# Layer 0 of a four-layer network: the output projection of a chunk and the power of its norm, issued half a turn sooner

## The chip, the cores and the metric

The kernel runs on one core of a Trainium2 chip. A core has five engines that run side by side, each with its own queue: PE (TensorE, matrix products; its weight loads are listed apart as PEld), DVE (VectorE), ACT (ScalarE), POOL (GpSimd) and SP (SyncE, which here only issues DMAs). Engines wait for one another through semaphores. The metric is the device time of one execution in microseconds (us).

## The reference, cut to what matters

The network takes x of shape 16 x 64 x 64 x 256 (16 images of 4096 pixels with 256 channels) and adds four layers to it, one after the other, each as `x = x + layer(group_norm(x))`. The change lies in layer 0, which is a linear attention:

```python
qkv = jnp.einsum('bhwc,cf->bhwf', x, Wqkv)            # x is the group-normed input
q = jax.nn.softmax(q, axis=-3); k = jax.nn.softmax(k, axis=-2)
context = jnp.einsum('bdnh,benh->bdeh', k, v)         # per head
out = jnp.einsum('bdeh,bdnh->benh', context, q)
out = jnp.einsum('bhwc,cf->bhwf', out, Wout) + bout   # the output projection
out = (out - mean(out)) * rsqrt(var(out) + 1e-6) * ln_scale + ln_bias
```

The mean over the 256 output channels is taken out of `Wout` and `bout` beforehand, so the norm of the projection needs only the mean of the squares, a power of -1/2, and a scaling. Layers 1 to 3 are not touched.

## The kernel before, in words

**Tiles and turns.** An image is cut into 8 chunks of 512 pixels (`NCH`, `CT`), and the 256 attention channels into two halves `hf`. Layer 0 is one loop of turns (line 565): turn n treats image i, half hf and chunk t, with n = 16 i + 8 hf + t, and after the last of these 256 turns there are 16 more that finish the last image. A turn computes q, k and v of its chunk and half (`attended`). The images are overlapped: while (i, hf) is in `attended`, the softmax and the context of the half before it are worked off by generators in the list `chains` (`context`, `weighted`, `gate1`, `norm0`), which `step()` advances five times a turn. `output` multiplies the context into the weighted q in parts that are due in turns t = 3 to 7.

**The projection.** The turns with hf = 1 also project one chunk of the image before (`projected0`, job "x1"). So 8 turns of 16 carry a projection, 128 in the layer; the last image's chunks are projected two to a turn after the last q turn. One projection is:

- 8 products of `o` with `wo` into the PSUM tile `py` (line 424; each is two PE instructions, 16 in all);
- DVE adds `bout`, which gives `y` (line 429);
- ACT squares `y` in four quarters, with a sum of each (line 433);
- DVE scales the four sums and adds epsilon, `ss` (line 434); POOL raises it to -1/2, `rsy` (line 436);
- ACT scales `y` by `rsy`, four instructions (line 439);
- PE transposes `y` into two tiles `pt` (line 444; 16 instructions); ACT applies scale and bias, `yT` (line 448); DVE adds the input and takes maximum and statistics (lines 451 and 455). A store of the result is queued for the next turn.

`projected0` is a generator with a `yield` between these pieces. The loop advances it at fixed points. Call the turn in which a chunk's projection begins k. At the start of turn k the generator is made and run to its first `yield` (lines 588 to 591). In `between(0)` of turn k, which `attended` calls after the q product and the first half of the k and v products, the loop runs it on (lines 603 and 604). At the start of turn k+1 it is run on once more (lines 583 and 584), and in `between(0)` of turn k+1 for the last time (lines 601 and 602).

**PSUM.** Tag `mm` has two buffers of two banks: `pkv` (k and v), `py`, and `px` (line 502, the transposes of `mapped`, in some turns only) take them in turn. Tag `tr` has three one-bank buffers, for `pq`, `po` and `pt`. Tag `sm` has one, for the small products of the chains. In SBUF, `y` has three buffers, which it shares with the tile `mx` of the maximum tree in `context`.

**Order.** There is no hand-written instruction order. The framework lays out each engine's instructions at build time: the order of the text is the priority, and an instruction whose inputs its cost model holds for late lets a later one pass. On the chip each engine keeps the order laid out. The trace shows both: six of the sixteen instructions of `py` sometimes run ahead of the transposes `pt` of the chunk before, which the text has first.

Of the kernel before, what the change touches and what calls it, by code (L numbers as in the profile page):

```python
# [36 lines left out]
def network(ctx: ExitStack, tc: tile.TileContext, a: dict, out: bass.AP):  # L37
# [142 lines left out]
    with ExitStack() as st:  # L180
# [232 lines left out]
        def projected0(i, ch):  # L413


            if ch == 0:
                st1[i] = wk.tile([P, 2, NCH, 6], F32, tag="st1", name="st1")
                mxs[i] = wk.tile([P, 2, NCH], F32, tag="mxs", name="mxs")
            x1 = loaded.pop(("x1", i, ch))
            yield  # L420
            py = mm.tile([P, 4, C], F32, tag="mm", name="py")
            for q in range(4):
                for hf in range(2):
                    nc.tensor.matmul(  # L424
                        py[:, q, :], lhsT=om[i, hf][:, :, ch * 4 + q], rhs=wo[:, hf, :],
                        start=(hf == 0), stop=(hf == 1),
                    )
            y = wk.tile([P, 4, C], F32, tag="y", name="y", bufs=3)
            nc.vector.tensor_tensor(y, py, bout.unsqueeze(1).broadcast_to([P, 4, C]), ALU.add)
            ss = small.tile([P, 4], F32, tag="ss", name="ss")  # L430
            sq = wk.tile([P, C], F32, tag="sq", name="sq", bufs=1)
            for q in range(4):
                nc.scalar.activation(sq, y[:, q, :], AF.Square, accum_out=ss[:, q : q + 1])
            nc.vector.tensor_scalar(ss, ss, 1.0 / C, LN_EPS, ALU.mult, ALU.add)
            rsy = small.tile([P, 4], F32, tag="rsy", name="rsy")
            nc.gpsimd.tensor_tensor(rsy, ss, mhalf, ALU.pow)
            yield
            for q in range(4):
                nc.scalar.activation(y[:, q, :], y[:, q, :], AF.Copy, scale=rsy[:, q : q + 1])
            yield  # L440
            for h in range(2):
                pt = tr.tile([P, CT], F32, tag="tr", name="pt")
                for q in range(4):
                    nc.tensor.transpose(
                        pt[:, q * P : (q + 1) * P], y[:, q, h * P : (h + 1) * P], ident
                    )
                t = wk.tile([P, CT], F32, tag="t", name="yT", bufs=4)
                nc.scalar.activation(
                    t, pt, AF.Identity, bias=lnb[:, h : h + 1], scale=lns[:, h : h + 1]
                )  # L450
                nc.vector.tensor_tensor_reduce(
                    x1[:, h], t, x1[:, h], 1.0, -3.0e38, ALU.add, ALU.max,
                    accum_out=mxs[i][:, h, ch : ch + 1],
                )
                nc.vector.bn_stats(st1[i][:, h, ch, :], x1[:, h])
            stores.append(
                (x1_d[i, :, :, ch * CT : (ch + 1) * CT].rearrange("h p t -> p h t"), x1)
            )
            if ch == NCH - 1:
                chains.append(gate1(i))  # L460
# [104 lines left out]
        for n in range(LAST + 16):  # L565
# [22 lines left out]
            for job in work:  # L588
                if job[0] == "x1":
                    projecting.append(projected0(*job[1:]))  # L590
                    next(projecting[-1])
# [1058 lines left out]
```

## Time and profile before

| | us |
|---|---|
| median of three runs (8559.8 to 8580.07) | 8560.48 |
| the profiled execution, its own time | 8603.53 |
| its span, first to last instruction | 8601.7 |
| layer 0 in it (the last transposes of the last image's chunks are still running at 3096) | about 3110 |

| Engine | busy us in the span | share |
|---|---|---|
| PE | 6924.3 | 80% |
| PEld | 5146.2 | 60% |
| DVE | 6022.7 | 70% |
| ACT | 4835.8 | 56% |
| POOL | 3054.3 | 36% |

The median and the profiled execution differ by 43 us (0.5%). A profile page gives busy time per engine; what stands behind a waiting engine is read from the list of waits, in which a line says who waited for whom, for how many us in total, how often, and how long at most. A line of the timeline gives start, duration, engine, line, operation, the tiles written and read, the number of merged instructions, and in brackets the engine's idle time before it with what ended it. In the rows by stretches, each engine has its busy time in the stretch and the number of its instructions; then come the granted TensorE clock as a share of full speed, the share of DMA engines in use and the GB/s moved.

### The profile page before, as it was taken

Reading aid. Unit: us, or ns where it says so; the run is one execution under the profiler, and the core shown is the slowest. Engines: PE = TensorE matmul, PEld = TensorE weight load, DVE = VectorE, ACT = ScalarE, POOL = GpSimd, SP = SyncE. Lnnn points to the kernel's source line nnn. Section 1 sums busy time; section 2 is a strip of 40 time slices with the busy share of each in tenths; the row PEclk is TensorE's granted clock in tenths of the full one; section 3 lists DMA queues with packets and bytes.
Section 4 is the critical chain, followed back from the end, with each engine's and each line's share of the span. In section 5 each row is a group of like instructions: output and inputs, shape, how many; then the busy total and the mean of one; then the engine's idle time right before and its main releaser. Section 6 shows DMA issues by size and latency. Waiting matters only on the chain. (4 is left out here: it accounts for less than half of the span.)

```text
span 8601.7 us, 215728 instructions
## 1 busy us (share of the span) xinstructions
PE 6924.3 (80%) x88348; PEld 5146.2 (60%) x88348; DVE 6022.7 (70%) x7839; ACT 4835.8 (56%) x11136; POOL 3054.3 (36%) x2154
## 2 busy tenths in 40 slices
PE   7888888888888776477777777778588888888888
PEld 5666666666666542254555555555376767777776
DVE  6777777777766757499999999999744444444444
ACT  3555555555555536666666656665355555555554
POOL 1222222222222200367777777777611112111112
PEclk9999999999999868799888888889799999999999
DMA  6543333443333327756767677676578878888887
GB/s 221 180 141 133 133 128 133 142 137 130 130 113 108 101 80 244 234 188 230 241 230 239 229 232 236 228 240 195 173 222 257 248 243 255 252 258 252 252 256 241
DMA packets 1081775, 1695.70 MB, mean 197 GB/s; under 512 B 138834, under 2 KB 684963, under 8 KB 1079635
## 3 DMA queue, kind: packets, MB, share of 16 engines
q1 hardware_dynamic: 1080786, 1681.90, 60.7%
q8 instruction: 696, 11.40, 0.6%
q14 instruction: 293, 2.39, 0.1%
HBM read 1234.54 MB, written 469.76 MB: 198 GB/s over the span
## 5 line engine op out<-in xcount | busy, mean ns | idle before, releaser
L1107 DVE TENSOR_TENSOR pd<-xs,pw 128x1152 f32<-128x1152 f32 x1024 | 1305.3, 1346 | 5.3 <-ACT xs L1088 5.3
L1367 PE MATMUL pk<-rt,span 64*128 64x176 f32 x12288 | 1179.9, 328 | 51.3 <-issue 44.9
L1122 POOL TENSOR_TENSOR pd<-pd 128x2048 f32<-128x2048 f32 (+2 forms) x384 | 1066.8, 2778 | 314.6 <-DVE pd L1107 294.5
L1377 ACT ACTIVATE wm<-pk,spanb 128x176 f32<-128x176 f32 x2560 | 847.0, 425 | 554.8 <-PE pk L1367 551.5
L1453 POOL TENSOR_TENSOR ex<-ex,rx 128x192 f32<-128x192 f32 (+2 forms) x768 | 436.3, 571 | 1855.3 <-DVE ex L1446 1152.3
L1367 PEld LDWEIGHTS pk<-rt,span 64*128 64x128 f32 x12288 | 969.4, 191 | 128.2 <-issue 69.8
L292 PE MATMUL pkv<-wq,xn 128*128 128x256 f32 x4096 | 1000.8, 390 | 49.4 <-DVE isq L93 27.6
L1446 DVE SCALAR_TENSOR_TENSOR ex<-pa,msk,ex 128x192 f32<-128x192 f32 x704 | 294.0, 418 | 1056.9 <-ACT ex L1445 984.2
L292 PEld LDWEIGHTS pkv<-wq,xn 128*128 128x128 f32 x4096 | 792.2, 196 | 280.5 <-issue 154.0
L375 POOL TENSOR_TENSOR qa<-qa,mq 128x1024 f32<-128x1024 f32 x256 | 493.7, 1950 | 1295.0 <-DVE mq L387 633.8
L1433 PE MATMUL pa<-wm,xw 126*32 126x48 f32 x45056 | 762.9, 214 | 221.7 <-issue 179.8
L1382 DVE TENSOR_TENSOR wm<-pk,spanb 128x704 f32<-128x704 f32 x896 | 793.8, 888 | 187.6 <-PE pk L1367 185.7
L1433 PEld LDWEIGHTS pa<-wm,xw 126*32 126x32 f32 x45056 | 626.7, 111 | 411.5 <-issue 332.8
L1038 PE MATMUL px<-x2p,wis 128*128 128x512 f32 x1024 | 581.7, 717 | 196.1 <-ACT c L1136 130.2
L1084 PE MATMUL pt<-ident,pad 128*128 128x128 f32 x4608 | 613.6, 287 | 129.0 <-ACT rt L1062 76.4
L1084 PEld LDWEIGHTS pt<-ident,pad 128*128 128x128 f32 x4608 | 522.8, 147 | 287.9 <-ACT rt L1062 97.2
L1088 ACT COPY xs<-pt 128x512 f32<-128x512 f32 x1152 | 591.4, 601 | 138.5 <-PE pt L1084 129.8
L1258 DVE TENSOR_REDUCE x<-pd 128x512 f32<-128x4608 f32 x128 | 633.4, 4948 | 1.9
L280 PE MATMUL pq<-xn,wq 128*128 128x512 f32 x1024 | 525.3, 629 | 29.0 <-ACT xn L165 22.6
L424 PE MATMUL py<-wo,o 128*128 128x256 f32 x2048 | 533.0, 409 | 4.2 <-DVE maps L510 1.9
L1445 ACT ACTIVATE ex<-pa,msk 128x192 f32<-128x192 f32 x704 | 299.8, 426 | 413.0 <-PE pa L1433 219.4
L424 PEld LDWEIGHTS py<-wo,o 128*128 128x128 f32 x2048 | 488.2, 309 | 30.3 <-issue 5.6
(233 smaller groups left out, 11870.8 us busy)
## 6 DMA issues: line engine op xcount, KB each, us to landing
xw<-strips SPq DMA_DIRECT2D x1408, 256.0 KB
xn<-in_x SPq DMA_DIRECT2D x256, 512.0 KB
x_d<-x SPq DMA_DIRECT2D x256, 512.0 KB
xin<-in_x SPq DMA_DIRECT2D x128, 512.0 KB
x<-in_x SPq DMA_DIRECT2D x128, 512.0 KB
xm<-x_d SPq DMA_DIRECT2D x128, 512.0 KB
x<-x_d SPq DMA_DIRECT2D x128, 512.0 KB
x<-x_d SPq DMA_DIRECT2D x256, 256.0 KB
```

Of the source, the lines that this page charges most:

```text
L292: nc.tensor.matmul(pkv[:, q], lhsT=xn[:, h, q * P : (q + 1) * P], rhs=wq[:, h, f0 + P : f0 + 384], start=(h == 0), stop=(h == 1),)
L424: nc.tensor.matmul(py[:, q, :], lhsT=om[i, hf][:, :, ch * 4 + q], rhs=wo[:, hf, :], start=(hf == 0), stop=(hf == 1),)
L1038: nc.tensor.matmul(px, lhsT=w[:, h, fh * P : (fh + 1) * P], rhs=x2[:, h], start=(h == 0), stop=(h == 1),)
L1084: nc.tensor.transpose(pt[:, k, h * P : (h + 1) * P], lines[:, h, rc * 4 + e + k, 2 * j : 2 * j + P], ident,)
L1088: nc.scalar.copy(xs[:, e : e + 2, j, :], pt)
L1107: nc.vector.tensor_tensor(pd[:, r].rearrange("p (g f) k -> p g f k", f=16), run[:, oh * 9 * P : (oh + 1) * 9 * P].rearrange("p (g f k) -> ...
L1122: nc.gpsimd.tensor_tensor(pd[..., 0:n], pd[..., 0:n], pd[..., n : 2 * n], ALU.add)
L1258: nc.vector.tensor_reduce(x3[:, :, P:C], pd1, AX.X, ALU.add)
L1367: nc.tensor.matmul(pkv[:, b, m], lhsT=span[half, first + gg, s0 : s0 + P], rhs=rto[half, o // 4 * 2 + m, :], start=True, stop=True,)
L1377: nc.scalar.activation(dst[:, m // 2, m % 2], pkv[:, m // 2, m % 2], AF.Identity, bias=spanb[:, g0 + m : g0 + m + 1],)
L1382: nc.vector.tensor_tensor(dst, pkv, spanb[:, g0 : g0 + 4].rearrange("p (b m) -> p b m", b=2).unsqueeze(3).broadcast_to([P, 2, 2, NTL]), AL ...
L1433: nc.tensor.matmul(pav[p0 : p0 + 32, :, tj * TC : (tj + 1) * TC].rearrange("c g (w v) -> c g w v", v=2), lhsT=xw[0:TILE_IN, k, tj, 32 * q ...
```

## The change

In `projected0` the first `yield`, between taking the loaded input and the products into `py`, is removed, and a second `yield` is put behind the power. So the products, the addition of `bout`, the squares, `ss` and `rsy` are issued at the start of turn k, after the chains' first step, after the scaling of the chunk before and after the first transposition `qT` of the turn, but before the q, k and v products of the turn. The advance in `between(0)` of turn k then does nothing. Scaling (start of turn k+1) and transposes (`between(0)` of turn k+1) stay where they were. No instruction is added, removed or resized.

```diff
@@ -417,7 +417,6 @@
                 st1[i] = wk.tile([P, 2, NCH, 6], F32, tag="st1", name="st1")
                 mxs[i] = wk.tile([P, 2, NCH], F32, tag="mxs", name="mxs")
             x1 = loaded.pop(("x1", i, ch))
-            yield
             py = mm.tile([P, 4, C], F32, tag="mm", name="py")
             for q in range(4):
                 for hf in range(2):
@@ -434,6 +433,7 @@
             nc.vector.tensor_scalar(ss, ss, 1.0 / C, LN_EPS, ALU.mult, ALU.add)
             rsy = small.tile([P, 4], F32, tag="rsy", name="rsy")
             nc.gpsimd.tensor_tensor(rsy, ss, mhalf, ALU.pow)
+            yield
             yield
             for q in range(4):
                 nc.scalar.activation(y[:, q, :], y[:, q, :], AF.Copy, scale=rsy[:, q : q + 1])
```

## The prediction, made before the result was known

> **What bounds the kernel now.** I read the busy times by stretches first, because the page's shares are means over four layers and the change touches only the first.
>
> ```profile
> 320.00:800.00 480.00, 409.58 (x2849) 303.12 (x2847) 363.04 (x559) 267.03 (x470) 111.43 (x71) 0.95 0.46 152
> 800.00:2800.00 2000.00, 1747.03 (x12045) 1313.88 (x12046) 1448.38 (x2220) 1131.26 (x2086) 450.71 (x298) 0.95 0.38 128
> 2962.00:3125.00 163.00, 101.01 (x648) 78.50 (x647) 119.87 (x204) 72.64 (x167) 29.16 (x20) 0.74 0.37 122
> 3125.00:8601.00 5476.00, 4271.03 (x70106) 3159.99 (x70104) 3774.76 (x4383) 3129.49 (x8019) 2369.06 (x1702) 0.90 0.72 231
> ```
>
> After the start, layer 0 is PE's: in 2000 us of its middle PE is busy 1747 us (87%), DVE 72%, ACT 57%, POOL 23%, and DMA engines are 38% in use. What can be gained is PE's idle 253 us there. The last row, 5476 us of layers 1 to 3, is out of reach of the change. The list of PE's waits in the same 2000 us says what the idle time is:
>
> ```profile
> PE pt L444 <- ACT y L439: 96.5, 71, 2.7
> PE pk L331 <- DVE mx L315: 36.5, 11, 3.4
> PE pctx L350 <- issue: 25.8, 21, 2.6
> PE pkv L292 <- DVE isq L93: 21.8, 8, 3.2
> ```
>
> The largest wait, 38% of the idle time, is that of the transposes of the projection for the scaled y. The view of tile y gives it for the whole layer: 148.0 us in 106 waits, of which 30.0 lie before 800 us and 19.6 after 2962. For its cause I read the timeline of one ordinary turn with a projection (idle time in brackets).
>
> ```profile
> 1221.92 1.21 DVE L429 TENSOR_TENSOR y<-py,bout 128x1024 f32<-128x1024 f32 x1
> ...
> 1223.83 0.42 ACT L433 ACTIVATE sq<-y 128x256 f32<-128x256 f32 x1
> ...
> 1226.80 0.19 ACT L433 ACTIVATION_READ_ACCUMULATOR sq<-y 128x1 f32 x1
> ...
> 1227.10 0.17 DVE L434 TENSOR_SCALAR ss<-ss 128x4 f32<-128x4 f32 x1 [3.97 <-ACT sq L433]
> ...
> 1227.34 1.27 POOL L436 TENSOR_TENSOR rsy<-ss,mhalf 128x4 f32<-128x4 f32 x1 [10.96 <-DVE ss L434]
> 1227.44 0.60 PE L424 MATMUL py<-wo,o 128*128 128x256 f32 x2
> ...
> 1228.65 1.71 ACT L439 ACTIVATE y<-y,rsy 128x256 f32<-128x256 f32 x4 [0.82 <-POOL rsy L436]
> ...
> 1229.21 0.84 PE L444 MATMUL pt<-ident,y 128*128 128x128 f32 x4 [1.17 <-ACT y L439]
> ```
>
> It is one chain over four engines: py ends on PE at 1221.6, then addition, squares, sums, power, first scaling, and the first transpose starts at 1229.2, 7.6 us later. PE has only 6.4 us of other work to put in between (1221.6 to 1228.04), so it stands still for 1.17 us. At the change of image the chain is longer:
>
> ```profile
> 1264.49 2.29 DVE L387 TENSOR_REDUCE mq<-qa 128x64 f32<-128x2048 f32 x1 [3.34 <-ACT qa L284]
> ...
> 1266.69 0.16 DVE L434 TENSOR_SCALAR ss<-ss 128x4 f32<-128x4 f32 x1
> ...
> 1266.86 1.91 POOL L375 TENSOR_TENSOR qa<-qa,mq 128x1024 f32<-128x1024 f32 x1 [12.98 <-DVE ss L434]
> ...
> 1268.73 1.19 POOL L436 TENSOR_TENSOR rsy<-ss,mhalf 128x4 f32<-128x4 f32 x1
> ...
> 1270.51 1.44 PE L444 MATMUL pt<-ident,y 128*128 128x128 f32 x6 [2.40 <-ACT y L439]
> ```
>
> Here the sums lie behind a maximum of `weighted`, which itself waited for the q copy, and the power behind a subtraction of `weighted` on POOL. PE waits 2.4 us, and 2.7 us again for the next chunk. PE's waits for the scaled y in one image are 0.9 us (from 1178 to 1206), 3.7 (1206 to 1256) and 5.1 (1256 to 1291): 9.7 us.
>
> **What the Trainium skill says.** "Perfetto Trace Analysis", section Optimization Strategy: find the gaps on the engine that limits, see which semaphore ends them, and make that dependency start sooner. That is what the change does to the largest gap above. "TensorE: Matmul & The Clock Gate", section Architectural detail: ACT and DVE are strict first-in first-out, and PE can pull only weight loads ahead. The trace agrees: the sums at 1266.69 did not pass the maximum ahead of them, and PE stood still at 1229.21 with products of py queued behind the transposes. Same page, section What's actually happening: the array's clock is throttled by default and activity releases the throttle. The trace shows 1.00 granted from 1206 to 1256, where waits are near 1 us, and 0.92 from 1256 to 1277. So I expect no loss of clock from shorter gaps, and count no gain. "SBUF — State Buffer", section on its two separate sides: DVE and GpSimd share a port pair, held for whole instructions. The sums took 1.09 us at 1285.69, beside a subtraction on POOL, against a median of 0.169.
>
> **The change part by part.** Nothing is added or removed. Moved, 128 times: 16 py instructions (3.84 us of PE in a row), the addition (1.21), four squares with their reads (4 x (0.42 + 0.19) = 2.4 us of ACT), the sums (0.17) and the power (1.0 to 1.3 us of POOL). No DMA moves: the loads and stores of a turn are issued before all of this, the store of x1 comes from the last piece, which stays, and SP's queue is passed by nothing.
>
> *Removed wait.* In an ordinary turn PE's order becomes py(k), pq(k), first half of pkv(k), po, pt(k-1), second half of pkv(k), then py(k+1), pq, pkv, po, pt(k). Between the end of py(k) and pt(k): 1.88 + 1.89 + 1.02 + 1.44 + 1.89 + 3.84 + 1.88 + 1.89 + 1.02 = 16.8 us, less some 0.17 us of overlap at each of 8 joints, 15.4 us. The chain needs 7.6. The spare 7.8 us also covers a POOL pair of `weighted` (3.8 us). Before, the same sum was 1.2 us short. At the change of image no py(k+1) follows, which leaves 15.4 - 3.8 = 11.6 us; there the addition at 1278.39 took 11.0 us to the transpose at 1289.36, so this wait ends only just, and I do not count it fully.
>
> *Moved work and who is behind it.* On PE, pq(k) and pkv(k) come 3.84 us later in their turn. In a turn's middle this costs nothing: PE is the limit and total work is unchanged. On ACT, the squares may now precede the q copy (2.4 us at most). That copy frees a `tr` buffer, needed two tiles later, after pkv and po (2.9 us of PE): hidden; without that cover, up to 1.4 us a turn. On DVE the addition waits for py at the turn's head, with qT and `weighted` behind it. DVE is busy only 5.6 of 12 us in such a turn (1218 to 1230), which hides this. The power passes `weighted`'s second pair of subtractions on POOL, which at most makes that pair 1.3 us later. For buffers: y lives 19 us instead of 15 in turns of 12.2, so two are live and three exist. py(k) reuses py(k-1)'s bank pair, free for most of a turn; pkv(k) now gets 3.84 us more for the copies of pkv(k-1). In the three turns at hf = 1 that border on px, py needs the pair that the k and v copies free: bounded by 0 and the 3.1 us that pkv waits there today (1167.82); I take no change.
>
> *What is late next.* Within an image, nothing near: turns of hf = 0 with no chain in them run without PE waits. At the change of image, `context` and `gate1`: DVE is busy 32.8 of 39.3 us from 1277.4 to 1316.7, and PE waits there for mx, gn_d and pctx whatever the projection does. Some of the 5.1 us will come back as those waits. For it speaks that the squares no longer hold DVE up in the tree of `context` (0.99 us of idle, then 1.09 us of sums at 1285.69).
>
> *Sum.* The 148.0 us split as the image did, apart from the tail's 19.6 (128.4 = 49 + 67 + 12): of the 49 in ordinary turns I take 90%, 44; of the 67 at the change of image 65%, 44; of the 12 in the first turns of hf = 1, where DVE is the limit (28.8 of 30 us busy from 1160 to 1190), a third, 4; of the tail's 19.6, where chains over all engines set the pace, 40%, 8. Together 100 us. The profiled execution would go from 8603.5 to about 8503, and the median from 8560.5 to about 8460 (the 43 us between them stay).
>
> **The rivals.**
>
> *All of it and more*: every wait for y goes (148) and the context tree, freed of 2 us a change of image, gains 15 x 2 = 30: up to 178 us, 8382. For it: the slack of 7.8 us. Against: DVE at 83% at the change of image.
>
> *The gain comes back at the change of image*: only the ordinary turns' 44 remain, or fewer: 8516. For it: the single `sm` bank strings context, gate1 and norm0 together, and PE waits for them already.
>
> *Slower, by the last q of an image.* Place: the turn with t = 7, hf = 1. py now goes ahead of pq there, so the last q copy comes 3.84 us later, and with it the 36 us of `weighted` (1264.5 to 1300.4), which qT needs at 1301.45. Its two maxima (2 x 2.28 = 4.6 us of DVE) slide from a stretch where DVE idled 3.3 and 2.5 us into the one that is 83% busy. Price: up to 8.4 us an image, and the 5.1 are not gained. Against the 4.6 us gained elsewhere in the image this loses 3.8, over 15 images 57: 8617. It decides from 4.6 us of added length on. Against it: PE itself reaches that turn's end 2.4 us sooner, and qT's consumer po waits for the context until 1311.3, 10 us after the first qT.
>
> *It does not do what it says*: the planner's order differs from the text already (py ahead of pt at 1227.44), and could stay in effect what it was: 8560. Against: an earlier place is a higher priority, and py's inputs are ready.
>
> **How the numbers follow.** A measurement of this kernel tells about 0.3%, 26 us, from no change. Forecast (60 to 150 us gained) 0.64; all and more 0.08; gain comes back (15 to 60 gained) 0.14, of which 0.01 lies within 26 us; slower 0.09; no effect 0.05. So faster 0.85, same 0.06, slower 0.09. The likeliest time is 8460, its own range 8410 to 8500. The range for 8 in 10 takes in both neighbouring cases: 8385 to 8550. It leaves out the slower case and most of that without effect.
>
> **What would show it.** Right: PE's wait for the scaled y falls from 148 us to under 30; ordinary turns shorten from 12.2 to 11.1 us and 13.1 to 12.5; DVE's wait of sums for squares remains, but costs PE nothing; layers 1 to 3 keep their 5476 us. The change-of-image term is wrong if waits for mx, gn_d or pctx grow by more than 2 us an image. The forecast is wrong if pq or py itself shows a new wait at the head of the turn (for k and v copies, or for the last o), or if qT or po wait for `weighted` in turns 3 and 4.

## The result, and the profile after

| | before | after |
|---|---|---|
| median of four runs, us | 8570.27 | 8516.74 |
| lowest to highest | 8559.8 to 8580.45 | 8500.31 to 8523.61 |
| profiled execution, its span | 8601.7 | 8498.4 |
| end of layer 0 in it (last instruction of line 451) | 3099.7 | 3026.7 |

The ratio is 0.9935, with a 95% interval from 0.9912 to 0.9958: 54 us faster, 36 to 75 by the interval. The two profiled executions differ by 103 us, but only 73 of these lie in layer 0. The rest, 5502 against 5472 us of layers 1 to 3, has the same instructions in both; in the eight experiments below it was 5480 to 5495. So I take it for the spread of single executions.

First the rows by stretches of the changed kernel (columns as before: each engine's busy time, then clock, DMA share and GB/s). Line numbers in the projection, from the products to the power, are one lower than before (423 for 424); in the experiments they shift by a few lines too.

```profile
320.00:800.00 480.00, 405.94 (x2929) 305.27 (x2931) 380.97 (x562) 261.36 (x456) 106.06 (x70) 0.94 0.46 149
800.00:2800.00 2000.00, 1734.94 (x12395) 1327.40 (x12385) 1535.27 (x2280) 1150.57 (x2118) 447.56 (x301) 0.94 0.39 131
2896.00:3052.00 156.00, 89.63 (x617) 69.43 (x615) 118.37 (x199) 66.19 (x151) 26.71 (x19) 0.73 0.37 120
3052.00:8498.00 5446.00, 4282.68 (x70116) 3184.98 (x70116) 3780.02 (x4386) 3127.74 (x8021) 2370.06 (x1702) 0.89 0.72 232
```

In the middle 2000 us PE executed 12395 instructions instead of 12045, 3% more, yet it is no busier: 1735 us after 1747. Its idle time is 265 us, where it was 253. The gain is not in PE's idle total. The list of PE's waits there shows that the waits have been exchanged:

```profile
PE pq L280 <- DVE xn L166: 56.8, 22, 5.0
PE pk L331 <- DVE mx L315: 54.3, 21, 3.5
PE pctx L350 <- DVE isq L93: 38.4, 11, 3.5
PE pctx L350 <- issue: 28.4, 23, 2.1
PE py L423 <- DVE maps L510: 22.1, 10, 3.2
PE px L505 <- ACT xm L172: 20.1, 11, 2.3
PE pt L444 <- DVE o L409: 15.5, 29, 1.2
```

The wait for the scaled y, 96.5 us before, is not among them; in the whole layer it is 8.4 us (148.0 before). New at the head are waits of the q product for its normed input (3.6 us before), of the context product for the norm chain (2.1 before), and more for the maximum tree (36.5 before). All three are for DVE. The first two before:

```profile
PE pq L280 <- DVE xn L166: 3.6, 10, 2.2
PE pctx L350 <- DVE isq L93: 2.1, 6, 0.3
```

To place this, I cut the profile into turns, each ending with the last of its 16 `pkv` products on PE, and took the mean over 13 images (the third to the fifteenth). A turn holds the same work in both kernels.

| us per image | before | after | difference |
|---|---|---|---|
| turns 0 to 5 (hf = 0, behind the change of image) | 59.17 | 65.77 | +6.59 |
| turns 6 and 7 | 15.52 | 15.52 | 0.00 |
| turns 8 to 10 (first three of hf = 1) | 48.78 | 46.97 | -1.82 |
| turns 11 to 14 (ordinary turns with a projection) | 50.47 | 44.51 | -5.95 |
| turn 15 (last chunk) | 15.81 | 12.53 | -3.28 |
| image | 189.76 | 185.30 | -4.46 |

Outside these 13 images the first two gain 12.0 us, the last one 4.8, and the tail behind its last q turn loses 1.7: 13 x 4.46 + 12.0 + 4.8 - 1.7 = 73.1, the difference in layer 0.

An ordinary turn of the changed kernel, from its timeline:

```profile
1200.54 1.02 PE L408 MATMUL po<-qT,cs 128*128 128x512 f32 x2
...
1201.40 1.04 PE L444 MATMUL pt<-ident,y 128*128 128x128 f32 x8
...
1202.23 0.17 DVE L433 TENSOR_SCALAR ss<-ss 128x4 f32<-128x4 f32 x1 [2.96 <-ACT sq L432]
...
1202.48 1.01 POOL L435 TENSOR_TENSOR rsy<-ss,mhalf 128x4 f32<-128x4 f32 x1 [9.47 <-DVE ss L433]
...
1203.52 0.91 ACT L439 ACTIVATE y<-y,rsy 128x256 f32<-128x256 f32 x2 [1.39 <-POOL rsy L435]
...
1204.00 3.73 PE L423 MATMUL py<-wo,o 128*128 128x256 f32 x16
```

The transposes at 1201.40 follow po without a gap, and those for the chunk just summed at 1202.23 come a turn later. The sums still wait 3 us for the squares, which costs PE nothing.

The change of image, on PE and then on DVE:

```profile
1261.03 1.02 PE L280 MATMUL pq<-xn,wq 128*128 128x512 f32 x2
1262.21 0.35 PE L134 MATMUL pg<-gn_mv,gmat 128*128 128x2 f32 x2 [0.16 <-DVE ka L341]
1267.52 2.07 PE L280 MATMUL pq<-xn,wq 128*128 128x512 f32 x2 [4.96 <-DVE xn L166]
1269.39 0.51 PE L151 MATMUL pv<-gn_d,gmat 128*128 128x2 f32 x2
1273.38 0.83 PE L350 MATMUL pctx<-va,ka 128*32 128x33 f32 x37 [3.49 <-DVE isq L93]
```

```profile
1238.33 2.24 DVE L387 TENSOR_REDUCE mq<-qa 128x64 f32<-128x2048 f32 x1
1240.49 2.01 DVE L451 CUSTOM_DVE_ANT_0 x<-yT,x 128x512 f32<-128x512 f32 x1
...
1255.40 2.27 DVE L383 TENSOR_REDUCE mq<-qa 128x64 f32<-128x2048 f32 x1
1257.59 4.47 DVE L341 TENSOR_TENSOR ka<-ka,pb 128x2048 f32<-128x2048 f32 x2
...
1262.67 2.27 DVE L383 TENSOR_REDUCE mq<-qa 128x64 f32<-128x2048 f32 x1
1264.87 1.60 DVE L146 TENSOR_TENSOR gn_d<-gn_mv,gn_m 128x2 f32<-128x2 f32 x1
...
1266.93 0.53 DVE L166 TENSOR_SCALAR xn<-xn,gn_m,gn_r 128x512 f32<-128x512 f32 x1
```

PE stands 5 us before 1267.52 for a norm that lies on DVE behind both sums of the softmax of q (line 383), the subtraction from k between them (line 341) and the chain's small operations. From the end of turn 15 (1240.2) to 1273.7 DVE is full. The row of this stretch in the changed kernel, and the first sum in the kernel before:

```profile
1240.20:1273.70 33.50, 21.57 (x101) 13.91 (x102) 33.42 (x48) 22.55 (x27) 14.53 (x8) 0.86 0.36 126
```

```profile
1273.77 2.29 DVE L383 TENSOR_REDUCE mq<-qa 128x64 f32<-128x2048 f32 x1 [2.53 <-ACT qa L380]
```

In the kernel before, this sum ran ahead of the end of turn 15 (1277.5), in a stretch where DVE still idled; here it lies 15 us behind it.

### The profile page after: what moved, and what is told of

Same layout as the page of the kernel before. It is cut to its first block, busy times and chain, and to the rows that moved or that the text cites. A ratio compares the mean times of both kernels' runs of the same rounds, so it can differ in the third digit from the quotient of the medians.

```text
span 8498.4 us, 215779 instructions
## 1 busy us (share of the span) xinstructions
PE 6860.2 (81%) x88348; PEld 5148.9 (61%) x88348; DVE 6094.1 (72%) x7839; ACT 4825.8 (57%) x11136; POOL 3041.0 (36%) x2154
## 3 DMA queue, kind: packets, MB, share of 16 engines
q14 instruction: 292, 2.39, 0.1%
## 5 line engine op out<-in xcount | busy, mean ns | idle before, releaser
L292 PE MATMUL pkv<-wq,xn 128*128 128x256 f32 x4096 | 967.6, 382 | 16.0 <-ACT va L301 16.0
L292 PEld LDWEIGHTS pkv<-wq,xn 128*128 128x128 f32 x4096 | 770.8, 192 | 228.7 <-issue 101.4
```

The lines of the kernel that those rows point to most:

```text
L292: nc.tensor.matmul(pkv[:, q], lhsT=xn[:, h, q * P : (q + 1) * P], rhs=wq[:, h, f0 + P : f0 + 384], start=(h == 0), stop=(h == 1),)
```

## Experiments

The turns of the profiles, as in the table above, in us per image. The column "15 and 0-5" is the change of image, the last one the period from image to image.

| kernel | turns 0-5 | 8-10 | 11-14 | 15 | 15 and 0-5 | image |
|---|---|---|---|---|---|---|
| before | 59.17 | 48.78 | 50.47 | 15.81 | 74.98 | 189.76 |
| after | 65.77 | 46.97 | 44.51 | 12.53 | 78.30 | 185.30 |
| e1, all but the last chunk | 62.33 | 47.30 | 44.66 | 12.54 | 74.87 | 182.35 |
| e2, last chunk alone | 66.05 | 46.50 | 49.77 | 13.22 | 79.28 | 191.07 |
| e3, last chunk behind q | 60.99 | 47.64 | 44.62 | 12.65 | 73.64 | 181.43 |
| e4, all behind q | 61.13 | 46.84 | 43.56 | 12.50 | 73.63 | 179.56 |
| e5, before, no maximum | 63.51 | 43.98 | 49.64 | 12.18 | 75.70 | 184.85 |
| e6, after, no maximum | 59.27 | 42.61 | 44.64 | 11.33 | 70.61 | 173.39 |
| e7, before, no scaling | 61.82 | 47.90 | 44.03 | 11.98 | 73.80 | 181.25 |
| e8, as e4, scaling early | 61.87 | 47.14 | 43.56 | 12.50 | 74.37 | 180.59 |

Two theories were to be told apart. A: the last chunk's products now stand ahead of the last q product of an image, so the softmax of q comes late and slides into the stretch where DVE is full. B: the chains at the change of image take their time in any case, and what PE gains ahead of them it waits off there.

**e1: all chunks but the last.**

```diff
             x1 = loaded.pop(("x1", i, ch))
+            if ch == NCH - 1:
+                yield
...
             nc.gpsimd.tensor_tensor(rsy, ss, mhalf, ALU.pow)
-            yield
+            if ch < NCH - 1:
+                yield
             yield
```

> The half-turn shift for chunks 0 to 6 of an image; the last chunk (t = 7) as before. Mean period of an image in the profiles: 189.8 us before, 185.3 after the change. Theory A (what is lost at the change of image comes from the last chunk: its products stand ahead of the last q product, so the softmax of q comes late and slides into the stretch where DVE is full): the turns 0 to 5 of the next image go back to about their 59 us of before (66 after the change), the ordinary turns keep their gain, period 179 to 181, some 70 to 90 us less in all than the changed kernel. Theory B (the strung-up chains of the change of image take their time whatever PE does, and any time PE gains ahead of them is waited off there): turns 0 to 5 stay at about 64 to 66, period 185 to 187.

Measured: 8465.72 us, ratio to the kernel before 0.9886 (0.9866 to 0.9907), period 182.35. It beats the changed kernel by 3 us an image, all of it in turns 0 to 5 (62.33 for 65.77). But those do not return to 59: turn 15 keeps its gain of 3.3 us, and turns 0 to 5 give exactly that back (74.87 for the two together, 74.98 before). So both theories hold in part. A: the place of the last chunk costs 78.30 - 74.87 = 3.4 us an image. B: what PE gained in turn 15 is waited off, if not all of it for the chains.

```profile
PE pk L331 <- DVE mx L315: 30.8, 10, 3.5
PE pt L447 <- ACT y L442: 22.6, 10, 3.1
PE pq L280 <- DVE xn L166: 22.1, 10, 2.2
PE pv L151 <- DVE gn_d L148: 20.5, 12, 2.1
PE pkv L292 <- DVE y L430: 19.2, 10, 1.9
```

These are PE's waits in 1800 us of e1 (800 to 2600). The wait for scaled y is back once an image, for the last chunk; the wait of q for its normed input is 2.2 us each where the changed kernel has up to 5.0. The last line is 1.9 us an image that e1 alone has: in turn 0 the k and v products wait for the addition to the last chunk's `py`. So e1 does not show by itself how much of what is given back is due to the chains.

**e2: the last chunk alone**, the two conditions exchanged.

> The half-turn shift for the last chunk of an image alone, chunks 0 to 6 as before. Theory A: turn 15 gains little, turns 0 to 5 grow by about 6 us, period 192 to 195 us, slower than before by 30 to 80 us in all. Theory B: turn 15 and the wait behind it gain up to 2.5 us and the chains give it back: 188 to 190, no change that can be measured.

Measured: 8603.79 us, ratio 1.0053 (1.0038 to 1.0068), period 191.07. Slower than before by some 40 us (8564.94 was the median of the kernel before in the same round). This part of the change, by itself, is a loss. Turns 0 to 5 grew by 6.9 us, as theory A has it. The period is below its 192 to 195 because turns 8 to 15 gained 5.6 us under an altered layout of instructions.

**e3: the last chunk's products behind q.** A hook is called in `attended` after the q product and its copy.

```diff
+            first()
             pkv = mm.tile([P, 4, C], F32, tag="mm", name="pkv")
...
-                    next(projecting[-1])
+                    if not ("q" in todo and job[2] == NCH - 1):
+                        next(projecting[-1])
+
+            def first():
+                for job in work:
+                    if job[0] == "x1" and job[2] == NCH - 1:
+                        next(projecting[-1])
```

> The change as it is, but in the turn of the last chunk its products are issued behind the q product and the q copy of that turn, ahead of k and v. Theory A: the softmax starts as early as before and the power is still early, so both waits of the change of image go: turns 0 to 5 at 57 to 60 us, period 176 to 180, the fastest of these. Theory B: about the changed kernel's 185.

Measured: 8454.51 us, ratio 0.987 (0.9854 to 0.9887), period 181.43. All that differs from the changed kernel in the text is which of q product and projection comes first in one turn of sixteen, and the change of image falls from 78.30 to 73.64 us. That settles the place of the loss. My 176 to 180 was too low, again by the part that theory B keeps: turn 15 gains 3.2 us, and turns 0 to 5 cost 1.8 more than before.

**e4: every chunk behind q.** As e3, without the condition on the chunk.

> As the run before it, in every turn: products of the projection behind the q product and copy, ahead of k and v. The chain to the transposes loses 1.9 us of its spare 7.8, so ordinary turns stay without waits (10.5 and 11.8 us). Theory A: period as in the run before it, 176 to 180. Theory B: about 185.

Measured: 8433.37 us (8425.85 to 8455.08), ratio 0.9853 (0.9839 to 0.9868), period 179.56, inside what theory A gave. This version beats both kernels: 1.5% faster than before, where the change gives 0.65%. Its list of PE's waits (800 to 2600 us):

```profile
PE pk L332 <- DVE mx L316: 32.3, 11, 3.4
PE pq L280 <- ACT xn L165: 30.2, 20, 3.2
PE pctx L351 <- issue: 24.1, 23, 1.6
PE py L424 <- DVE isq L93: 22.8, 8, 3.5
PE pv L151 <- DVE gn_d L148: 17.0, 12, 1.5
PE pt L445 <- ACT y L440: 15.1, 10, 1.5
```

The q product waits no longer for DVE's half of the norm but, more briefly, for ACT's.

The traces also show which step of the softmax the loss goes with. The first of its two sums on DVE begins, in the mean over the 13 images, 3.7 us before the end of turn 15 in the kernel before, 15.1 us behind it in the changed kernel and 15.0 in e2; in e1 it is 3.5 us behind, in e3 and e4 0.8 and 0.3 us before. The second sum is as late in e3 and e4 (22.0 and 22.6 us behind) as in the changed kernel (22.8), and costs nothing there. So it is the lateness of the first sum that goes with a long change of image.

**e5 and e6: the load taken off.** In both kernels the maximum of the q softmax and its subtraction are left out of `weighted`.

```diff
             for k in range(2):
-                nc.vector.tensor_reduce(mq[:, halves[k]], qa[:, halves[k]], AX.X, ALU.max)
-                scaled(k, mq, ALU.subtract)
                 yield
```

> The kernel before, with the maximum of the q softmax and its subtraction left out (the exponential is taken of q itself, the same function without its guard): 2 x 2.28 us less on DVE and four 1.95 us operations less on POOL per half. It is the partner of the next run. The change of image (turn 15 and the next turns 0 to 5, 74.9 us before) gets shorter, to 66 to 73 us.

> The changed kernel with the same left out. Theory A1 (the late q product costs time because the softmax slides into a stretch where DVE is full): with that load off, the change of image is no longer than in the run before it (within 1 us; the changed kernel is 3.3 us longer than the kernel before with the load on), and the period is at least 8 us less than that run's. Rival A2 (the late q product costs by itself, through its copy and PE's order): the change of image stays 3 us longer than in the run before it, and the period is some 4.5 us less, as with the load on.

Measured: 8507.8 us for e5 and 8342.74 for e6, periods 184.85 and 173.39. With the load off, the same change brings 11.5 us an image instead of 4.5, and the change of image gets shorter by 5.1 us instead of longer by 3.3. In e6 the first sum begins 2.2 us before the end of turn 15. That fits A1, in which the late q product costs through what the softmax then meets and not by itself. It has two limits. The maximum and the subtractions go together, on DVE and on POOL, so the exponentials also start sooner: the pair does not tell a full DVE from a longer path. And e5 is not a clean partner. What I expected of it was missed: its change of image did not get shorter (75.7 us). It waits 3.5 us for scaled y in turn 1 (2.6 before) and 2.0 for the norm chain in turn 3 (0.3 before). Of the 5.1 us by which e6 is shorter, up to 3.5 may be that wait for y.

**e7: the wait for y by itself.** The kernel before, without its scalings.

```diff
-            for q in range(4):
-                nc.scalar.activation(y[:, q, :], y[:, q, :], AF.Copy, scale=rsy[:, q : q + 1])
             yield
```

> The kernel before with the four scalings of y left out (the projection is not normed), so that the transposes wait for the addition only; order of the text as before. Theory P (the transposes were held by the scaled quarters twice: 1.0 us of listed wait and another 0.7 us in which their pairs ran at the pace of the scalings): ordinary turns 11 and 12 go from 12.3 to 10.5 us, as in the changed kernel. Rival Q (the 0.7 us is the price of products mixed in between the transposes): they stay at 11.2 or more.

Measured: 8459.91 us; turns 11 and 12 take 10.57 us. Before, a turn with two parts of `output`, then the same in e7:

```profile
1238.82 1.88 PE L408 MATMUL po<-qT,cs 128*128 128x512 f32 x4
1241.43 1.75 PE L444 MATMUL pt<-ident,y 128*128 128x128 f32 x8 [0.74 <-ACT y L439]
1243.02 3.83 PE L424 MATMUL py<-wo,o 128*128 128x256 f32 x16
```

```profile
1198.94 1.88 PE L408 MATMUL po<-qT,cs 128*128 128x512 f32 x4
1200.66 1.04 PE L442 MATMUL pt<-ident,y 128*128 128x128 f32 x8
1201.54 3.84 PE L424 MATMUL py<-wo,o 128*128 128x256 f32 x16
```

Eight transposes took 1.75 us before, the 1.71 us of the four scalings, and 1.04 us when they wait for nothing. These 0.7 us stand in the profile as busy time. They could have been read off the weight loads, which in the 2000 us of before waited for scaled y for 160.1 us where the products waited 96.5:

```profile
PEld pt L444 <- ACT y L439: 160.1, 182, 3.1
```

The surplus of 63.6 us over the 87 projections in that stretch is 0.73 us each. Theory P holds. (e7 also takes 2 us a projection off ACT; but the changed kernel, which keeps that work, has the same turns of 10.5 us.)

**e8: e4, with the scaling half a turn sooner too.**

```diff
             nc.gpsimd.tensor_tensor(rsy, ss, mhalf, ALU.pow)
             yield
-            yield
             for q in range(4):
                 nc.scalar.activation(y[:, q, :], y[:, q, :], AF.Copy, scale=rsy[:, q : q + 1])
             yield
+            yield
```

> As the fourth run (all projections behind the q product), and the scaling half a turn sooner too, in the second part of its own turn. Where scaled y is still late there (1.5 us of wait in turn 0) the period falls by up to 1.5 us to 178 to 179. Rival: the scalings get in the way of the k and v copies on ACT, and the period stays at 179.6 or rises.

Measured: 8447.88 us (8441.61 to 8462.89), period 180.59. No gain: the wait in turn 0 is 1.50 us as in e4 (1.51), so the place of the scaling in the text is not what makes y late there. What makes it late stays open.

## Why the prediction was right, and where it was not

The forecast of faster, with its range, held: 8516.74 lies in 8385 to 8550. But its 100 us were 54, below the 60 to 150 of the forecast itself and among the 15 to 60 of the rival whose gain comes back at the change of image. Even the time is the one given to that rival (8516). That is luck: more was won inside the image and more lost at its change than it had. In the forecast, too, errors of both signs met. By the table of turns, the terms inside the image were 68 us too small and those of the change of image and the tail 104 too large.

*Removed wait: right.* The wait for scaled y fell from 148.0 to 8.4 us, under the 30 named, by the mechanism named; the 7.8 us of spare time were enough.

*Ordinary turns: the size was off, and too small.* The term was 44 us (90% of 49), with turns of 11.1 and 12.5 us; measured are 10.5 and 11.8, and 5.95 us an image, 89 over 15 images. The missed part is the 0.7 us by which each set of transposes ran at the pace of the scalings. My sum took the wait from the products' list alone, and PE's idle 253 us for all that could be gained; e7 shows the rest.

*First turns of hf = 1: too small as well.* Taken at 4 us; 1.82 an image, 27 over 15. This was not tried apart.

*Change of image: the step that failed.* I took 44 us of gain (65% of 67), 2.9 us an image. Measured are -3.28 in turn 15 and +6.59 in turns 0 to 5, a loss of 3.3 us an image or 50 over 15. Nearly all of the 6.59 is idle time of PE: 9.8 us in turns 0 to 5 before, 16.2 after. Two things make up the loss.

- Of the waits for y, 5 us an image, little can be kept there. e3, e4 and e7 take most of them away without delaying the last q product, and come to 73.6, 73.6 and 73.8 us for turns 15 and 0 to 5, 1.2 to 1.4 under the 74.98 of before. The rest returns as other waits. That is B.
- The rival's mechanism, py ahead of the last q product, at the place that it names, costs 4.7 us: 78.30 in the changed kernel, 73.64 in e3. Against e1, which leaves the last chunk as it was, it is 3.4.

The rival's price was up to 8.4 us, and it decided from 4.6 us of added length on; the 3.3 stayed below that. In the rest of the image 7.8 us were gained (5.95 + 1.82) where it had 4.6, so the whole stayed faster. Its path was near, not exact: both maxima still began inside turn 15 (5.4 and 1.9 us before its end, 12.9 and 8.5 in the kernel before), and what slid into the full stretch are the sums behind them. My argument against it, 10 us between the first qT and the context's end, looked at qT and po alone. The chain lost its time earlier: on DVE, where the softmax's sums stand ahead of the norm that the next q product needs.

The sign named for this term came: the waits for `mx` and `gn_d` and that of `pctx` for the norm chain grew by 4 us an image together (3.1 to 5.1, 1.2 to 0.3, 0.3 to 3.3), where 2 were named. So did a new wait of pq, though for its normed input and not for the copies.

*The tail: wrong in sign.* Taken at 8 us of gain; it lost 1.7.

*Costed at nothing, and so it was, but for one:* py waits 22.1 us for its bank pair where pkv waited 21.8 (the product first at the head of turn 8 has changed, not the wait); the last o holds up no py; the granted clock in layer 0's middle is 0.94 for 0.95; layers 1 to 3 have no change that their spread would let one see. The exception is small: the transposes of turns 13 to 15 now wait for an `o` (15.5 us in the 2000 us, 1.4 us an image), whose reading of po frees one of the three `tr` buffers. In e4 that wait is gone from turns 13 and 14.

One reading in the prediction is wrong, without consequence: what ran on POOL beside the sums at 1285.69 was a multiplication of `weighted`, issued after the reciprocal at 1284.15, and not a subtraction.

## What to carry to other kernels

When work is moved ahead in a turn, look in the last turn before a change of stage for what it has been moved ahead of: there a product that feeds a long chain pays for the delay (4.7 us an image here), while in the other seven turns with a projection the same order cost 1.9 us together (e4 against e3). Move the work behind that product, and the gain of the other turns is kept without the loss. And read the waits of the weight loads beside those of the products, since a product that keeps pace with its producer shows as busy.

## What was not expected of the hardware

DVE's time for the same instructions depends on what runs beside it. Over the 13 images the durations of DVE's instructions add up to 151.99 us an image before and 156.95 after, with no instruction more. Much of that is line 451, before and then after:

```profile
L451 DVE CUSTOM_DVE_ANT_0 x<-yT,x 128x512 f32<-128x512 f32 x174 | 117.0, 689 | 118.0 <-ACT yT L448 118.0
```

```profile
L451 DVE CUSTOM_DVE_ANT_0 x<-yT,x 128x512 f32<-128x512 f32 x174 | 150.4, 880 | 90.3 <-ACT yT L448 90.3
```

Two of it took 2.01 and 2.39 us at 1240.49 and 1242.43, beside three subtractions on POOL from 1240.04 to 1246.6. In the 13 images of the changed kernel the 26 executions that began while such a subtraction ran took 2.20 us in the mean, the other 182 took 0.69. In e6 the order is the other way round: 12 executions began 0.08 us before a multiplication on POOL, and took 0.69 us, while the multiplication took 2.38 instead of 1.9. So here the one that began second was the one held up. That agrees with what the Trainium skill ("SBUF — State Buffer", section "SBUF: two separate sides") says of the port pair that DVE and GpSimd share: it is held for a whole instruction. With the subtractions left out (e5 and e6, where the maxima are gone too) the two kernels' DVE time is the same, 143.22 and 143.43 us an image. It does not tell the variants apart: e1 has 156.46 us and e4 156.16.
